# First layer's feed-forward by pairs of chunks, and the queries' weights loaded by blocks

## The chip, the cores and the metric

The kernel runs on one core of a Trainium2 chip, in one launch. All data are float32. The metric is the device time of an execution in microseconds (us). A profiled execution gives a trace besides: every instruction of every engine with its start and its duration. The engines are called by their short names here: PE (TensorE, the matrix products; PEld is its loading of weights), DVE (VectorE), ACT (ScalarE), POOL (GpSimd) and SP (SyncE, which mostly issues DMAs).

## The reference, cut to what matters

Two layers work on x of 4 x 512 tokens with 512 features. The change lies in the first one. Its normalised input xn goes two ways: through an attention that is a sequential scan over minibatches of 16 tokens (each step updates a small weight matrix by a gradient), and through a gated feed-forward. Both are added to x. The second layer has an attention with compressed keys and queries ("latents") and a feed-forward of four experts; it is not touched by the change itself.

```python
# first layer, attention: 32 heads of 16, one step for each of 32 minibatches
Z1 = xk @ W1_s + b1_s
grad = _ln_fused_l2_bwd(Z1, xv - xk, ln_w, ln_b)
Z1_bar = xq @ W1_s - eta_mb * Attn1 @ grad + b1_bar
W1_new = W1_s - (last_eta * xk).swapaxes(-1, -2) @ grad
# first layer, feed-forward: 512 -> 1408 -> 512
g = jnp.einsum('th,ih->ti', xf, gate_w) * gate_s
u = jnp.einsum('th,ih->ti', xf, up_w) * up_s
hdn = jax.nn.silu(g) * u
out = jnp.einsum('ti,hi->th', hdn, down_w) * down_s
# the whole
x = x + attention_0(xn) + ffn_0(xn)          # layer 0
x = x + attention_1(xn) + experts_1(xn)      # layer 1, with xn of the new x
```

## The kernel before

The first stage (some 930 us of the trace) does the whole first layer. It cuts the 512 tokens of each of the four batches into NCHUNK = 8 chunks of 64 tokens, so that a chunk has CW = 256 columns (64 tokens x 4 batches), and a chunk holds CH = 4 steps of the recurrence (NM = 32 steps in all, numbered n = 0 to 31 here).

The recurrence is the loop near the end of the stage (L781 to L797). Each step forms the products pz (first_product, L345) from the running weights, whose block-diagonal copy is wq_bd (L332). The gradient is a chain of small operations on DVE with a square and a square root on ACT (L354 to L390). Its result goes into g_bd (L395) for the products wacc that update the weights, and into gh (L421, POOL) for the products pso that give the step's output. The next step's pz needs wacc. All these PE products are short; in a step the gradient chain is what takes the time.

While that chain runs, PE gets other work. `work` is a chain of Python generators, one `between(ch)` for each chunk (L656 to L687). Each piece of work that such a generator emits gives back an estimate of its time, and `fill(us)` takes pieces until the estimates cover the given number of us. A step calls fill three times, with 11, 3 and 8 us (GAPS): before the update, before the output products, and after them. A further loop empties the generator as far as needed before the next chunk's first step, because that step needs the chunk's keys, tokens and queries (`done`). The order in which the program text emits instructions isn't the order that each engine gets: the framework's scheduler orders the instructions of an engine anew, by its own plan, when the program is built. Once built, the order on each engine is fixed.

The pieces of `between(ch)` are, in order:
- gate_up(ch, i) for 11 blocks of 128 hidden units (L465 to L481). Two weight tiles wg and wu of 256 KB each are loaded on SP (two buffers each). Four products of 256 columns each go into each half of the PSUM tile pf (ps_ff, two buffers). ACT makes sg = Silu of the first half (L477), DVE multiplies it with the other half into hid (L478). hid has one buffer.
- For the next chunk: norm_turn (transposes of the normalised rows into xT), keys, two token tiles (values and step sizes, stored as rows and read back as kv), and queries. keys and queries call `features` (L242), four output blocks of four products each; the queries' weights are one tile wq of 1 MB that stays in SBUF for the whole stage (L188).
- down(ch, u) for both halves of the chunk (L483 to L498): 11 products of 512 columns (pd) with one weight tile wd of 256 KB each, four buffers, loaded on SP.
- finish(ch - 1) (L545 to L606): gate the recurrence's outputs, norm them, project them, add everything up, norm again, transpose and store them (xe_d) for the second layer.

In the last chunk latent_operands, latent_rows and latents (L610 ff.) compute the second layer's latents: the normalised rows of chunks 0 to 5 are read back into the memory of wk, wv and wq (`latent_rows(k)`, L622 to L625), as soon as that memory isn't needed any more, those of chunks 6 and 7 stay in SBUF in xT tiles. After this stage come the expert feed-forward (L914 ff.; its weights gu and rows xe are issued on POOL at L927 and L931, more of them on SP) and the second attention, up to 2028 us.

Every f32 product leaves two records in the trace, so that counts of PE records are twice the counts of products.

## Time and profile before

| What | Value |
|---|---|
| three runs | 2028.45, 2035.72, 2035.77 us; median 2035.72 us |
| the profiled execution | 2030.29 us; span from first to last instruction 2028.3 us |
| mean granted TensorE clock | 0.998 |
| ACT busy | 863.2 us (43% of the span) |
| table loads of ACT in the first stage | 1.28 us each where they show |
| loads wg and wu (SP) | 88 each, 256 KB, 3.1 us from issue to landing (median) |
| loads wd (SP) | 176, 256 KB, 3.0 us |
| loads kv (POOL) | 32, 264 KB, 4.1 us |
| SP's data queue (q1) | 237.31 MB, 43.2% of 16 DMA engines |

How to read the profile: a row of the groups names line, engine, operation, `out<-in` by the program's names, tile sizes, the number of records, then the busy time in us and the mean duration in ns, then the idle time of the engine just before these instructions and what ended most of it. PE's products overlap, each is still draining when the next one streams, so that the mean of a record (388 ns) is longer than the distance between two of them. A row of the timeline begins with the start in us and the length of a run of like instructions; in brackets stands the idle time ahead of it and what released it. A row of the waits has the total in us, the number of waits and the longest.

Over the first stage, in slices of 100 us from the start, PE is busy for 89.1, 97.1, 95.0, 96.7, 94.5, 98.7, 97.8, 97.9 and 93.6 us.

### The profile page before, as it was taken

Reading aid. Unit: us, or ns where it says so; the run is one execution under the profiler, and the core shown is the slowest. Engines: PE = TensorE matmul, PEld = TensorE weight load, DVE = VectorE, ACT = ScalarE, POOL = GpSimd, SP = SyncE. Lnnn points to the kernel's source line nnn. Section 1 sums busy time; section 2 is a strip of 40 time slices with the busy share of each in tenths; the row PEclk is TensorE's granted clock in tenths of the full one; section 3 lists DMA queues with packets and bytes.
Section 4 is the critical chain, followed back from the end, with each engine's and each line's share of the span. In section 5 each row is a group of like instructions: output and inputs, shape, how many; then the busy total and the mean of one; then the engine's idle time right before and its main releaser. Section 6 shows DMA issues by size and latency. Waiting matters only on the chain.

```text
span 2028.3 us, 30787 instructions
## 1 busy us (share of the span) xinstructions
PE 1968.2 (97%) x10502; PEld 1245.2 (61%) x10502; DVE 1302.3 (64%) x2720; ACT 863.2 (43%) x1763; POOL 631.8 (31%) x707
## 2 busy tenths in 40 slices
PE   8999999999999999998999999999999999999999
PEld 6777676767676776744776445555555555555555
DVE  4546657575756574754654487777777777777773
ACT  2233343333343443422322365555555555555552
POOL 4334242434342433421001132223223232354320
PEclk9999999999999999999999999999999999999999
DMA  6757576646373655545831144344434443333332
GB/s 166 210 129 220 132 193 166 183 128 184 114 203 116 179 151 163 182 136 189 281 104 56 39 101 117 95 103 115 108 94 114 103 114 86 97 97 89 94 100 93
DMA packets 318472, 270.90 MB, mean 134 GB/s; under 512 B 87660, under 2 KB 239405, under 8 KB 317677
## 3 DMA queue, kind: packets, MB, share of 16 engines
q1 hardware_dynamic: 298080, 237.31, 43.2%
q0 software_dynamic: 8736, 26.31, 4.5%
q10 hardware_dynamic: 11500, 5.32, 0.9%
q8 instruction: 84, 1.38, 0.3%
q14 instruction: 72, 0.58, 0.1%
HBM read 174.18 MB, written 34.87 MB: 103 GB/s over the span
## 4 chain that ended last, share of the span: by engine, by line
PE 47%; DVE 1%; SPq 1%; ACT 1%; issue 0%; DMA 0%; DVEq 0%; ACTq 0%
PE sc L1134 9%; PE pc L1202 9%; PE pq L1124 7%; PE px L1245 5%; PE p L1245 4%; PE epg L969 3%; PE epo L1032 3%; PE pk L1116 2%; PE epu L969 1%; SPq L1194 1%; PE po L1302 1%; PE pw L868 1%; PE pvo L886 1%; ACT prob L1139 1%; ACT prob L1144 0%
## 5 line engine op out<-in xcount | busy, mean ns | idle before, releaser
L1139 ACT ACTIVATE prob<-sc,mx 128x512 f32<-128x512 f32 x256 | 174.3, 683 | 164.2 <-DVE mx L1136 159.4
L1134 PE MATMUL sc<-kT,qT 96*128 96x512 f32 x512 | 230.6, 592 | 1.6 <-DVE prT_head L1183 1.3
L1202 PE MATMUL pc<-prT,lv 128*128 128x512 f32 x488 | 219.6, 593 | 1.2 <-DMA prT<-tt 1.2
L1109 POOL TENSOR_TENSOR kT<-t_k,t_k 32x512 f32<-32x512 f32 x64 | 80.6, 1259 | 407.6 <-PE pq L1124 235.6
L1163 DVE STREAM_TRANSPOSE tt<-prob 128x512 f32<-128x512 f32 x248 | 170.3, 706 | 55.2 <-ACT prob L1144 43.7
L117 PE MATMUL pf<-xT,wg 128*128 128x256 f32 x704 | 173.7, 388 | 5.3 <-DMA wg<-in_wg 2.7
L1144 ACT ACTIVATE prob<-prob,sm 128x512 f32<-128x512 f32 x256 | 176.5, 713 | 0.0
L1124 PE MATMUL pq<-cq,uq 128*128 128x512 f32 x384 | 175.3, 592 | 0.8 <-ACT ctxT L1204 0.8
L1134 PEld LDWEIGHTS sc<-kT,qT 96*128 96x128 f32 x512 | 96.8, 190 | 124.1 <-issue 118.9
L1136 DVE TENSOR_REDUCE mx<-sc 128x1 f32<-128x512 f32 x256 | 168.0, 677 | 2.3 <-PE sc L1134 0.3
L117 PE MATMUL pf<-xT,wu 128*128 128x256 f32 x704 | 167.0, 380 | 1.3 <-DMA wu<-in_wu 1.3
L117 PE MATMUL pd<-wd,hid 128*128 128x512 f32 x352 | 165.9, 600 | 1.8 <-DMA wd<-in_wd 1.7
L117 PEld LDWEIGHTS pf<-xT,wg 128*128 128x128 f32 x704 | 132.1, 192 | 32.9 <-issue 7.6
L1202 PEld LDWEIGHTS pc<-prT,lv 128*128 128x128 f32 x488 | 92.5, 190 | 93.7 <-issue 90.7
L117 PEld LDWEIGHTS pf<-xT,wu 128*128 128x128 f32 x704 | 133.7, 190 | 20.4 <-DMA wu<-in_wu 2.3
L478 DVE SCALAR_TENSOR_TENSOR hid<-pf,us,sg 128x256 f32<-128x256 f32 x88 | 41.9, 477 | 153.9 <-ACT sg L477 153.5
L1124 PEld LDWEIGHTS pq<-cq,uq 128*128 128x128 f32 x384 | 72.8, 190 | 93.1 <-issue 81.5
L314 POOL TENSOR_SCALAR sk<-k,m 128x256 f32<-128x256 f32 x64 | 61.1, 964 | 179.8 <-PE pz L117 167.7
L421 POOL TENSOR_SCALAR gh<-grad,m 128x256 f32<-128x256 f32 x64 | 61.2, 967 | 153.2 <-DVE grad L390 135.5
L117 PEld LDWEIGHTS pd<-wd,hid 128*128 128x128 f32 x352 | 63.4, 190 | 60.5 <-issue 45.2
L1109 POOL TENSOR_TENSOR qT<-t_q,t_q 32x512 f32<-32x512 f32 x64 | 80.6, 1260 | 56.7 <-DVE t_q L1105 56.6
L477 ACT ACTIVATE sg<-pf,gs 128x256 f32<-128x256 f32 x88 | 41.5, 473 | 132.9 <-PE pf L117 132.5
(304 smaller groups left out, 3546.6 us busy)
## 6 DMA issues: line engine op xcount, KB each, us to landing
prT<-tt SPq DMA_DIRECT2D x992, 64.0 KB, 2.0
wd<-in_wd SPq DMA_DIRECT2D x176, 256.0 KB, 3.0
wg<-in_wg SPq DMA_DIRECT2D x88, 256.0 KB, 3.1
wu<-in_wu SPq DMA_DIRECT2D x88, 256.0 KB, 3.1
cq<-lat_d SPq DMA_DIRECT2D x48, 256.0 KB, 4.3
rows<-rows SPq DMA_DIRECT2D x128, 66.0 KB, 2.2
kv<-rows POOLq DMA_DIRECT2D x32, 264.0 KB, 4.1
gu<-in_gu SPq DMA_DIRECT2D x3, 2048.0 KB, 8.8
```

The costliest lines, as they stand in the source:

```text
L117: nc.tensor.matmul(out, lhsT=lhsT, rhs=rhs, start=start, stop=stop, skip_group_check=True)
L421: nc.gpsimd.tensor_scalar_mul(gh[:, :, h, :], g, m2[:, h : h + 1])
L969: nc.tensor.matmul(ps, lhsT=w[:, c, :], rhs=x[:, c], start=start and c == 0, stop=c == 1, skip_group_check=True)
L1109: nc.gpsimd.tensor_sub(t[RD:mid, :], t1[RD:mid, :], t2[RD:mid, :])
L1124: nc.tensor.matmul(pq, lhsT=w[f"uq{i}"][:, h, :], rhs=cqs[hg, b][:, i, :], start=(i == 0), stop=(i == nq - 1))
L1134: pin(nc.tensor.matmul(ps, lhsT=qT[:KQ, i * P : (i + 1) * P], rhs=kT[:KQ, :], start=True, stop=True))
L1136: pin(nc.vector.tensor_reduce(mx, ps, AX.X, ALU.max, negate=True))
L1139: pin(nc.scalar.activation(pr, ps, AF.Exp, bias=mx, scale=1.0, accum_out=sm))
L1144: pin(nc.scalar.mul(pr, pr, sm))
L1163: nc.vector.transpose(out=tt[:, :, :, i, :], in_=pr.rearrange("p (kb e j) -> p kb e j", e=2, j=K))
L1202: pin(nc.tensor.matmul(pc, lhsT=lv[:, b, k, :], rhs=prT[:, k, :], start=(k == 0), stop=(k == E - 1)))
L1245: nc.tensor.matmul(ps[:, q, :], lhsT=a[:, k, q * P : (q + 1) * P], rhs=w[:, k, :], start=start and k == 0 and q == 0, stop=k == 1, skip_gr ...
```

## The change

Gate and up products are made for a pair of chunks at a time, 512 columns a product. The tiles xT and hid hold pairs now (two xT buffers of a pair for three of a chunk; hid 22 KB a partition for 11), and pf is one tile for gate and one for up. An even chunk's `between` has nine of the pair's eleven blocks (FF_FIRST = 9), the projections of the next chunk and finish; an odd one has the other two blocks, the down products of both chunks, the projections and finish. The queries' weights no longer stay in SBUF: each chunk loads four blocks of 256 KB into the buffers of wg and wu, on SP. The buffers of kv and q1 go from three to two, those of sg from two to one. Of the latents, the rows of chunks 4 and 5 go into the memory of hid, and come last; the rows of chunks 6 and 7 share one tile.

```diff
--- before.py
+++ after.py
@@ -41,6 +41,8 @@
 
 INTER = 1408
 NI = INTER // P
+
+FF_FIRST = 9
 
 H, D, KVC, QC, RD = 16, 128, 128, 384, 64
 HALF = RD // 2
@@ -120,7 +122,7 @@
             return ps_pj.tile([P, 512], F32, tag="pj", name="pj")
 
 
-        xTs, xns = {}, {}
+        xTs, xTp, xns = {}, {}, {}
 
         def load_rows(t, src, ch, u):
             for b2 in range(2):
@@ -152,7 +154,9 @@
                 xns[ch, u] = xt
 
         def norm_turn(ch):
-            xTs[ch] = wk.tile([P, NC, CW], F32, tag="xT", name=f"xT{ch}", bufs=3)
+            if ch % 2 == 0:
+                xTp[ch // 2] = wk.tile([P, NC, 2, CW], F32, tag="xT", name=f"xT{ch}")
+            xTs[ch] = xTp[ch // 2][:, :, ch % 2, :]
             for u in range(2):
                 nc.scalar.copy(xTs[ch][:, :, u * P : (u + 1) * P], transposed(xns.pop((ch, u))))
                 yield 0.6
@@ -185,7 +189,6 @@
         gamma_row = wk.tile([P, HS], F32, tag="xr", name="gamma_row")
         gbeta_row = one.tile([P, HS], F32, tag="gbeta_row", name="gbeta_row")
         lrw = load(one, "lrw", [P, NC, P], a["lrw"].rearrange("(c p) m -> p c m", p=P))
-        wq_w = load(one, "wq", [P, NC, HS], a["wq"].rearrange("(c p) o -> p c o", p=P))
         one_row = one.tile([1, P], F32, tag="one_row", name="one_row")
         nc.vector.memset(one_row, 1.0)
 
@@ -239,21 +242,30 @@
         z_d = [dram.tile([NC * P, B, CT], F32, tag=f"z{ch}", name=f"z{ch}") for ch in range(NCHUNK)]
         k1, q1, rows = {}, {}, {}
 
-        def features(ch, w, got, tag, bufs):
-
-            t = got[ch] = wk.tile([P, NC, CW], F32, tag=tag, name=f"{tag}_{ch}", bufs=bufs)
+        def features(ch, w, got, tag):
+
+            t = got[ch] = wk.tile([P, NC, CW], F32, tag=tag, name=f"{tag}_{ch}", bufs=2)
             for be in range(NC):
                 pp = psum()[:, :CW]
+                wb = w(be)
                 for c in range(NC):
-                    mm(pp, w[:, c, be * P : (be + 1) * P], xTs[ch][:, c, :], c == 0, c == NC - 1)
+                    mm(pp, wb[:, c, :], xTs[ch][:, c, :], c == 0, c == NC - 1)
                 nc.scalar.copy(t[:, be, :], pp)
                 yield 1.72
 
         def keys(ch):
-            return features(ch, wk_w, k1, "k1", 2)
+            return features(ch, lambda be: wk_w[:, :, be * P : (be + 1) * P], k1, "k1")
 
         def queries(ch):
-            return features(ch, wq_w, q1, "q1", 3)
+            def block(be):
+
+                w = wk.tile([P, NC, P], F32, tag="wg" if be % 2 else "wu", name=f"wq_{ch}_{be}")
+                nc.sync.dma_start(
+                    out=w, in_=a["wq"].rearrange("(c p) o -> p c o", p=P)[:, :, be * P : (be + 1) * P]
+                )
+                return w
+
+            return features(ch, block, q1, "q1")
 
         def token_tile(ch, u):
             t = wk.tile([P, NS, RW], F32, tag="rows", name=f"rows_{ch}_{u}")
@@ -303,7 +315,7 @@
         def prepare(n):
 
             ch, i = divmod(n, CH)
-            kv = wk.tile([P, B, RW], F32, tag="kv", name=f"kv_{n}", bufs=3)
+            kv = wk.tile([P, B, RW], F32, tag="kv", name=f"kv_{n}")
             nc.gpsimd.dma_start(out=kv, in_=rows_d[ch][i].rearrange("s t b x -> (s t) b x"))
 
             def at(t, r):
@@ -462,21 +474,26 @@
         nc.gpsimd.dma_start(out=row["dsc"], in_=a["dsc"].unsqueeze(0))
         hid, yf = {}, {}
 
-        def gate_up(ch, i):
+        def gate_up(k, i):
+
             if i == 0:
-                hid[ch] = wk.tile([P, NI, CW], F32, tag="hid", name=f"hid_{ch}", bufs=1)
-            pf = ps_ff.tile([P, 2, CW], F32, tag="pf", name=f"pf_{ch}_{i}")
-            for j, nm in enumerate(("wg", "wu")):
-                w = wk.tile([P, NC, P], F32, tag=nm, name=f"{nm}_{ch}_{i}")
+                hid[k] = wk.tile([P, NI, 2, CW], F32, tag="hid", name=f"hid_{k}", bufs=1)
+            pf = []
+            for nm in ("wg", "wu"):
+                w = wk.tile([P, NC, P], F32, tag=nm, name=f"{nm}_{k}_{i}")
                 nc.sync.dma_start(out=w, in_=a[nm][i])
+                ps = ps_ff.tile([P, 2 * CW], F32, tag="pf", name=f"pf_{nm}_{k}_{i}")
+                pf.append(ps)
                 for c in range(NC):
-                    mm(pf[:, j, :], w[:, c, :], xTs[ch][:, c, :], c == 0, c == NC - 1)
-            if i < 10:
-                next(copies, None)
-            sg = wk.tile([P, CW], F32, tag="sg", name=f"sg_{ch}_{i}")
-            nc.scalar.activation(sg, pf[:, 0, :], AF.Silu, scale=gs[:, i : i + 1])
+                    mm(ps, w[:, c, :], xTp[k][:, c].rearrange("p h t -> p (h t)"), c == 0, c == NC - 1)
+                if i < 10:
+                    next(copies, None)
+                if nm == "wg":
+                    sg = wk.tile([P, 2 * CW], F32, tag="sg", name=f"sg_{k}_{i}", bufs=1)
+                    nc.scalar.activation(sg, ps, AF.Silu, scale=gs[:, i : i + 1])
+                    yield 3.43
             nc.vector.scalar_tensor_tensor(
-                hid[ch][:, i, :], pf[:, 1, :], us[:, i : i + 1], sg, ALU.mult, ALU.mult
+                hid[k][:, i].rearrange("p h t -> p (h t)"), pf[1], us[:, i : i + 1], sg, ALU.mult, ALU.mult
             )
             yield 3.43
 
@@ -487,7 +504,7 @@
             for i in range(NI):
                 w = wk.tile([P, HS], F32, tag="wd", name=f"wd_{ch}_{u}_{i}", bufs=4)
                 nc.sync.dma_start(out=w, in_=a["wd"][i * P : (i + 1) * P, :])
-                mm(pd, hid[ch][:, i, u * P : (u + 1) * P], w, i == 0, i == NI - 1)
+                mm(pd, hid[ch // 2][:, i, ch % 2, u * P : (u + 1) * P], w, i == 0, i == NI - 1)
                 if i in (3, 7):
                     yield 3.43
             t = wk.tile([P, HS], F32, tag="yf", name=f"yf_{ch}_{u}", bufs=4)
@@ -593,8 +610,9 @@
                 xns[ch, u] = xt
                 yield 4.4
             if ch >= NCHUNK - 2:
-                t = wk.tile([P, NC, CW], F32, tag="xT", name=f"xl_{ch}", bufs=3)
-                part = parts[ch] = t.rearrange("p c w -> p (c w)").rearrange("p (u c e x) -> p u c e x", u=2, c=NC, e=E)
+                if not last_rows:
+                    last_rows.append(wk.tile([P, 2, 2, NC, E, 32], F32, tag="xT", name="xl_last"))
+                part = parts[ch] = last_rows[0][:, ch % 2]
             for u in range(2):
                 if ch >= NCHUNK - 2:
                     xs = part[:, u]
@@ -605,7 +623,7 @@
                 yield 0.6
 
 
-        parts, lw = {}, []
+        parts, lw, last_rows = {}, [], []
 
         def latent_operands():
 
@@ -620,7 +638,12 @@
                 lw.extend(t[:, :, i * P : (i + 1) * P] for i in range(n // P))
 
         def latent_rows(k):
-            t = parts[2 * k, 2 * k + 1] = one.tile([P, 4, NC, E, 32], F32, tag=("wk", "wv", "wq")[k], name=f"xl_{k}")
+            if k < 2:
+                t = one.tile([P, 4, NC, E, 32], F32, tag=("wk", "wv")[k], name=f"xl_{k}")
+            else:
+                t = wk.tile([P, NI, 2, CW], F32, tag="hid", name=f"xl_{k}", bufs=1)
+                t = t[:, :4].rearrange("p i h t -> p (i h t)").rearrange("p (i c e x) -> p i c e x", i=4, c=NC, e=E)
+            parts[2 * k, 2 * k + 1] = t
             for i in range(4):
                 nc.sync.dma_start(out=t[:, i], in_=xe_d[4 * k + i])
 
@@ -656,36 +679,59 @@
         def between(ch):
 
             fin = finish(ch - 1) if ch > 0 else iter(())
-            if ch + 1 == NCHUNK:
+            k, odd = divmod(ch, 2)
+            proj = (keys(ch + 1), token_tile(ch + 1, 0), token_tile(ch + 1, 1), queries(ch + 1))
+            if not odd:
+                yield from norm_turn(ch + 1)
+                for i in range(FF_FIRST):
+                    yield from gate_up(k, i)
+                    if i == 3:
+                        yield from take(fin, 1)
+                if ch == 0:
+                    yield from finish_constants()
+                nxt = chain(*proj)
+                for j in range(6):
+                    yield from take(nxt, 2)
+                    yield from take(fin, 1)
+                yield from nxt
+                done.add(ch + 1)
+                yield from fin
+                if ch + 2 < NCHUNK:
+                    norm_rows(ch + 2)
+                return
+            last = ch + 1 == NCHUNK
+            if last:
                 latent_operands()
-            for i in range(NI):
-                yield from gate_up(ch, i)
-                if ch + 1 == NCHUNK and i in (2, 5, 8):
-                    latent_rows(i // 3)
-                if i == NI - 3:
-                    yield from take(fin, 1)
-            if ch == 0:
-                yield from finish_constants()
+                latent_rows(0)
+            for i in range(FF_FIRST, NI):
+                yield from gate_up(k, i)
+            if last:
+                latent_rows(1)
+            yield from down(ch - 1, 0)
+            yield from take(fin, 1)
+            dn = down(ch - 1, 1)
+            yield from take(dn, 2)
             nxt = iter(())
-            if ch + 1 < NCHUNK:
-                nxt = chain(
-                    norm_turn(ch + 1), keys(ch + 1), token_tile(ch + 1, 0), token_tile(ch + 1, 1), queries(ch + 1)
-                )
+            if last:
+                yield from dn
+                yield from fin
             else:
-                yield from fin
+                nxt = chain(norm_turn(ch + 1), *proj)
             for u in range(2):
-                dn = down(ch, u)
-                for j in range(3):
+                dn = chain(dn, down(ch, u))
+                for j in range(3 + (u == 0)):
                     yield from take(nxt, 2)
                     yield from take(dn, 1)
                     yield from take(fin, 1)
+                if u == 0 and ch + 2 < NCHUNK:
+                    norm_rows(ch + 2)
             yield from nxt
             done.add(ch + 1)
+            yield from dn
             yield from fin
-            if ch + 2 < NCHUNK:
-                norm_rows(ch + 2)
-            if ch + 1 == NCHUNK:
-                for key in sorted(parts, key=str):
+            if last:
+                latent_rows(2)
+                for key in ((0, 1), (2, 3), 6, (4, 5)):
                     yield from latents(key)
 
         def take(it, k):
```

## The prediction

> **What bounds the kernel now.** I read the page's busy times first, then the costliest groups, the waits of PE up to 930 us (the first stage), and last the PE, DVE and POOL timelines of single places.
>
> ```profile
> PE 1968.2 (97%) x10502; PEld 1245.2 (61%) x10502; DVE 1302.3 (64%) x2720; ACT 863.2 (43%) x1763; POOL 631.8 (31%) x707
> L117 PE MATMUL pf<-xT,wg 128*128 128x256 f32 x704 | 173.7, 388 | 5.3 <-DMA wg<-in_wg 2.7
> L117 PE MATMUL pf<-xT,wu 128*128 128x256 f32 x704 | 167.0, 380 | 1.3 <-DMA wu<-in_wu 1.3
> L117 PE MATMUL pd<-wd,hid 128*128 128x512 f32 x352 | 165.9, 600 | 1.8 <-DMA wd<-in_wd 1.7
> L478 DVE SCALAR_TENSOR_TENSOR hid<-pf,us,sg 128x256 f32<-128x256 f32 x88 | 41.9, 477 | 153.9 <-ACT sg L477 153.5
> ```
>
> PE is busy 97% of the span. The gate and up products (pf) and the down products (pd) hardly wait, and they are what PE does while the recurrence's gradient runs on DVE. So two things alone can move the time: how long PE needs for its products, and how much PE work stands ready inside each recurrence step. The waits show the second:
>
> ```profile
> PE pso L117 <- POOL gh L421: 5.6, 3, 2.7
> PE wacc L117 <- ACT g_bd L395: 3.5, 4, 1.6
> ...
> PE pf L117 <- DMA wg<-in_wg: 2.7, 2, 2.6
> PE pz L117 <- ACT wq_bd L332: 2.5, 2, 1.4
> ...
> PE pf L117 <- DVE hid L478: 2.2, 3, 1.1
> ```
>
> All waits of this view come to about 45 us, no more than that can be won by tidier waiting. Two steps of the recurrence are "thin", with less PE work than gradient; here they are as PE saw them:
>
> ```profile
> 263.60 0.48 PE L117 MATMUL pso<-a_bd,gh 128*32 128x68 f32 x17 [2.72 <-POOL gh L421]
> ...
> 266.78 1.08 PE L117 MATMUL pz<-wq_bd,sk 128*32 128x128 f32 x32 [1.40 <-ACT wq_bd L332]
> ...
> 268.24 1.99 PE L117 MATMUL pf<-xT,wg 128*128 128x256 f32 x8
> 270.07 1.89 PE L117 MATMUL pf<-xT,wu 128*128 128x256 f32 x8
> 271.80 1.89 PE L117 MATMUL pf<-xT,wg 128*128 128x256 f32 x8
> ```
>
> ```profile
> 701.98 1.08 PE L117 MATMUL pz<-wq_bd,sk 128*32 128x128 f32 x32
> ...
> 712.23 0.65 PE L117 MATMUL wacc<-g_bd,km 128*32 128x64 f32 x32 [1.61 <-ACT g_bd L395]
> ```
>
> From the end of pz (703.06) to wacc (712.23) is 9.2 us. DVE shows that this is the chain itself, with hardly a foreign operation in it:
>
> ```profile
> 703.13 0.42 DVE L356 TENSOR_REDUCE s<-pz 128x16 f32<-128x256 f32 x1
> ...
> 711.27 0.81 DVE L395 COPY g_bd<-grad 32x256 f32<-32x256 f32 x2
> ```
>
> In the thin step that ends at 263.6 the chain took 10.6 us, with two hid operations of the feed-forward (0.48 and 0.47 us) inside. I price it at 9.9, the middle, with 9.2 and 10.6 as ends.
>
> **Streaming.** Each f32 product has two records. In the fence that begins at 263.60, eight records of 256 columns follow eight others after 1.73 to 1.83 us (1.727 over the whole run of them), 0.216 us a record. For 512 columns:
>
> ```profile
> 303.61 3.60 PE L117 MATMUL pd<-wd,hid 128*128 128x512 f32 x8
> 307.04 0.59 PE L117 MATMUL pz<-gsum,bones 128*128 128x256 f32 x2
> ```
>
> Eight records take 3.43 us, 0.429 each. So a 512-wide product saves 2 x 1.727 - 3.43 = 0.024 us per four products; 88 such groups (four pairs, 11 blocks, two matrices) give **-2.1 us**. The Trainium skill (TensorE: Matmul & The Clock Gate, section "Back-to-back issue gap") has a sustained stream of load and matmul at about 81 ns for N = 128 and 131 ns for N = 512; drawn linearly, an estimate, 98 ns at 256. By that rule a 512 product costs 0.67 of two of 256, and the 173.7 + 167.0 us of pf would lose about 112 us. The row rules it out: here time goes with columns and the weight load (190 ns) is already under the 213 ns of the pass. I take -2.1, ends 0 and -4.
>
> **Thin steps (the largest term).** The change orders work anew: even chunks hold nine gate/up pairs, odd ones two, then 2 x 2 down tiles. I counted, in the built order of PE, the fill that stands between pz of each step and its first wacc, at 0.43 us a 512-wide record and 0.216 a 256-wide one, plus 0.6 for the queries' pso:
> - step 3: queries' blocks 2 and 3 (3.4) and four down products (3.4), 6.9; missing 9.9 - 0.6 - 6.9 = 2.4.
> - step 7: one block of queries (1.7) and eight transposes (1.0), 2.7; missing 6.6.
> - step 15: 8.6; missing 0.7.
> - step 28 (first of the last chunk): only the two 512-wide bones products, 1.7, because the next gate product stands behind wacc; missing 7.6.
>
> That is 17.3. After wacc there is nothing before the next pz in steps 3 and 7 (1.4 each, the wait in the line at 266.78) and 0.9 us in steps 11 and 15 (0.5 each): 3.8. Sum 21.1. The thin steps of before (2.72 + 1.40 above, 1.05 of another pz, 1.61) are gone, -6.8: **+14.3**. With 9.2 it is +11.5, with 10.6 about +17. All other steps keep 8.9 us or more of fill in both orders. These steps are late because the next minibatch needs wacc; nothing else is ready on PE.
>
> **Waits on gate loads and hid.** The waits of pf in this view (2.7 for wg, 1.3 for wu, 2.2 for hid, 0.4 for a buffer freed late behind xh, 6.6 in all) belong to blocks; half as many blocks give **-3.3** (0 to -6.6). A rule speaks against the wider operations: the Trainium skill (Perfetto Trace Analysis, "Optimizing Scalar/DVE Operations") says that where ScalarE or VectorE aren't saturated but make bubbles elsewhere, breaking instructions up may let work finish sooner. Silu and hid go from 0.47 us (their rows) to about 0.68 (the 128x512 rows of ACT in the attention). By the rule each pair would pay 0.2 us more bubble, 44 x 0.2 = +9. But the page shows hid waiting for sg 153.5 us in all and PE waiting for hid 2.2: a pf buffer comes free while PE streams 3.43 us of the other one, in both kernels. I take the row.
>
> **The start.** In the two orders, 6.9 us of pf stood among the startup's products before the first pz, now 1.0 us of transposes, so that the first pz comes 4.9 us earlier and about 1 us of cover is lost. **+1** (0 to +2).
>
> **Queries by blocks.** 32 loads of 256 KB are added, 88 gate/up loads go (176 to 88); all on SP's queue, which gets shorter (q1 is busy 43%). Block 0 is covered by some 7 us of token-tile products against a landing of 3.1. Cost 0; uncovered, 3 us per chunk. kv and q1 with two buffers in place of three: kv lands in 4.1 us and is asked for one step (some 25 us) ahead, so 0; if a load came a whole landing late each time it would be 30 x 4.
>
> **Down in long runs.** Odd chunks have up to 14 to 20 down products in a row. A product needs 0.857 us of PE and one 256 KB load; four buffers over 0.857 + 0.33 (issue) + 3.0 (landing) give 1.05 us each. Before, runs of 8 and 10 lost 0.9 and 1.8 us. **+3** (0 to +6).
>
> **Tail.** Rows 4 and 5 of the latents move into the hid tile and come last. The final norm's transposes lose 3.2 + 0.7 us of cover and 1.3 us of existing waits go: **+2.3**. The expert weights overlay the same memory, so they are moved as well:
>
> ```profile
> 910.97 0.75 POOL L927 DMA_DIRECT2D gu<-in_gu  x1
> ...
> 923.49 0.54 POOL L931 DMA_DIRECT2D xe<-xe_d  x1 [7.05 <-DMA gu<-in_gu]
> ```
>
> gu and 14 xe loads on POOL, and two xe with gu_1, dn and y behind them on SP, now wait for the last latent product; adding up the products that stand before it in both orders puts the last xe about 17.7 us later. PE needed them at 969.35; by the same count the first epg moves by 18.5 to 22 us (the sum below and the tail's own). **+1** (0 to +6).
>
> **Sum.** 14.3 - 2.1 - 3.3 + 1 + 3 + 2.3 + 1 = +16.2 us. The profiled run took 2030.29 us (span 2028.3 and 2.0 around it); so 2046.5. The median of the three runs, 2035.72, is 5.4 above the profiled run, the lowest 1.8 below, so a scatter of some 5 us lies on either side.
>
> **Rivals.**
> 1. *Evens out* (2032). The thin steps cost as before because chain and fill overlap better than counted, and the tail hides: half the thin term (+7), -2.1, -3.3, nothing else. For it: POOL and ACT have slack everywhere. Against: fill is counted from a fixed order.
> 2. *Faster* (2020). Half as many Silu and hid operations, each with its wait, and 65 table loads in place of 83 in the built order (1.28 us each in the trace) shorten the waits everywhere: half of the 38 us outside the thin steps go (-19), -2.1, thin steps at the short chain (+11.5): -9.6. It decides when over 22 us of the 45 go, or when the thin steps cost under some 2 us. Against: most of these 38 us are norms and loads that are not changed.
> 3. *Slower by much more* (2066). The tail's loads come too late for the experts: gu takes 12 us and xe 9 us to land; if the first expert product waits for both, +20 in place of +1. It decides from the point where xe issue later than 9 us before epg. The kv of the last chunk, needed about when its rows are stored (13.5 us against 14.3), would add here.
> 4. *The change doesn't do what it says*: the built order shows 512-wide products and single blocks; none given.
>
> **Numbers.** Forecast 0.56 (own range 2036 to 2060), evens out 0.18, faster 0.15, much slower 0.11. Half a per cent, about what a measurement can tell from no change, is 10 us. Slower: most of the forecast (0.52) and rival 3, 0.63; same: rival 1 and the forecast's edge, 0.22; faster 0.15. The range takes 2023 to 2064.
>
> **What will show it.** pf records of about 592 ns, spaced 0.43, 704 in all. Waits of wacc for g_bd (or pso for gh) of 6 to 8 us near the first chunk's end (step 7) and in step 28; pz for wq_bd 1.4. Waits of pd for wd of a few us. The issue of gu against the first epg. It is wrong if thin steps show no wait over 3 us, if pf's records are spaced under 0.4 us, or if waits of the unchanged norms grow.

## The result and the profile after

| Kernel | Median | Ratio to before, 95% interval |
|---|---|---|
| before | 2035.49 us (4 runs beside it) | 1 |
| changed | 2101.37 us (2099.95 to 2103.43) | 1.0334 (1.0322 to 1.0347) |

The change makes the kernel 3.3% slower, some 66 us, where 16 were forecast and 2064 was the upper end of the range. The profiled execution of the changed kernel took 2099.95 us (span 2098.2). In it the first expert product (epg) starts at 1038.33 us, in the kernel before at 969.35; these 69.0 us are practically the whole loss (the spans differ by 69.9). So nearly all of it lies in the first stage.

The profile page of the changed kernel, the rows that answer to those shown of before:

```profile
PE 1989.9 (95%) x9798; PEld 1122.0 (53%) x9798; DVE 1300.1 (62%) x2676; ACT 830.2 (40%) x1701; POOL 632.8 (30%) x707
...
PEclk9999989999999999899999999999999999999999
...
L119 PE MATMUL pd<-wd,hid 128*128 128x512 f32 x352 | 171.9, 612 | 16.3 <-DMA wd<-in_wd 11.1
L119 PE MATMUL pf_wg<-xT,wg 128*128 128x512 f32 x352 | 169.9, 627 | 12.8 <-ACT sg L493 12.8
...
L119 PE MATMUL pf_wu<-xT,wu 128*128 128x512 f32 x352 | 159.8, 597 | 2.0 <-DVE hid L495 2.0
```

Two things stand out. Idle time before pd has gone from 1.8 to 16.3 us, and pf now waits 12.8 us for Silu (sg), a wait that the list of before doesn't have. And the mean granted clock, 0.998 before, is 0.981 here. (The groups pf_wg and pf_wu have half the records, each twice as wide; the 597 ns of a pf_wu record is close to the forecast 592.)

The waits of PE up to 1000 us (total, number, longest):

```profile
PE pso L119 <- POOL gh L433: 24.9, 4, 14.2
PE pf_wg L119 <- ACT sg L493: 12.8, 3, 8.6
PE pd L119 <- DMA wd<-in_wd: 11.1, 12, 2.6
PE pj L119 <- ACT pn_sq L566: 8.4, 1, 8.4
PE pd L119 <- DVE yf L511: 5.2, 3, 3.0
...
PE pz L119 <- POOL wq_bd L328: 3.0, 1, 3.0
```

To split the 69.0 us I took the windows view in slices of 1 us up to the first epg, added up the part of each slice in which PE was idle, and, for the part in which it was busy, its length times (1 - granted clock):

| up to the first epg | before | changed | difference |
|---|---|---|---|
| PE idle | 46.9 us | 94.2 us | +47.3 |
| PE busy, lost to a lower clock | 3.3 us | 24.6 us | +21.3 |
| PE busy, the rest | 919.1 us | 919.6 us | +0.5 |
| sum, rounded | 969.35 us | 1038.33 us | +69.0 |

Two thirds are stalls, one third is time at a lower clock, which comes behind stalls. The PE work itself has not got shorter by being wider.

**Late operands from POOL.** The worst stalls stand in the first step of chunks 3, 5 and 7 (steps 12, 20, 28). Two names are needed for them: zb is the recurrence's output of the chunk before, stored as z and read back, and pn_sq is the first operation of its norm. Step 12 on PE, then on DVE, ACT and POOL:

```profile
392.80 1.08 PE L119 MATMUL pz<-wq_bd,sk 128*32 128x128 f32 x32
...
395.22 3.60 PE L119 MATMUL pf_wg<-xT,wg 128*128 128x512 f32 x8
398.65 3.60 PE L119 MATMUL pf_wu<-xT,wu 128*128 128x512 f32 x8
410.81 6.36 PE L119 MATMUL pf_wg<-xT,wg 128*128 128x512 f32 x8 [8.56 <-ACT sg L493]
```

```profile
402.75 0.18 DVE L379 TENSOR_TENSOR rl<-r,kv 128x16 f32<-128x16 f32 x1 [3.71 <-DMA kv<-rows]
...
406.93 0.90 DVE L407 COPY g_bd<-grad 32x256 f32<-32x256 f32 x2
```

```profile
406.85 1.06 ACT L566 ACTIVATE pn_sq<-zb 128x1024 f32<-128x1024 f32 x1 [3.16 <-DMA zb<-z]
407.93 0.83 ACT L407 COPY g_bd<-grad 32x256 f32<-32x256 f32 x2
408.77 1.28 ACT L493 ACT_TABLE_LOAD   x1
410.07 0.69 ACT L493 ACTIVATE sg<-pf_wg,gs 128x512 f32<-128x512 f32 x1
```

```profile
395.23 1.11 POOL L319 DMA_DIRECT2D kv<-rows  x2
396.39 0.84 POOL L328 COPY wq_bd<-q 32x256 f32<-32x256 f32 x2
402.39 0.76 POOL L468 DMA_DIRECT2D zb<-z  x1 [5.17 <-DMA z<-zch]
```

Read from the stall backwards. PE had fill in its queue (the next gate product), but no free pf buffer: Silu of the first was late. ACT hadn't been slow; in its order Silu stands behind pn_sq and the g_bd copies. (Silu's one buffer in place of two, which no run has alone, is not it: ACT waits for it 1.4 us in the whole stage.) The copies wait for DVE's gradient, and DVE stood for 3.71 us for kv; pn_sq waits for zb. The two came within a tenth of a us of each other (gradient 406.89, zb 406.85), so that here either alone would have held ACT nearly as long. Both loads come late from POOL: zb waits there for the landing of z, and kv was issued only at 395.23, while this step's pz had started at 392.80. The fence on ACT shows as well why fill in a queue isn't always fill: it needs buffers that come free on other engines.

In steps 20 and 28 the issues came at 631.63 and 867.88, 5.8 and 4.7 us after their pz, and DVE stood for 5.91 and 4.62 us. PE in steps 20 and 28, then POOL in step 28:

```profile
635.75 3.78 PE L119 MATMUL pj<-pn_sq,bones 128*128 128x512 f32 x4 [8.41 <-ACT pn_sq L566]
...
863.17 1.08 PE L119 MATMUL pz<-wq_bd,sk 128*32 128x128 f32 x32
...
880.78 0.32 PE L119 MATMUL pso<-a_bd,gh 128*32 128x68 f32 x1 [14.17 <-POOL gh L433]
```

```profile
864.47 1.82 POOL L326 TENSOR_SCALAR sk<-k,m 128x256 f32<-128x256 f32 x2 [1.63 <-PE pz L119]
866.24 1.69 POOL L328 COPY wq_bd<-q 32x256 f32<-32x256 f32 x4
867.88 1.16 POOL L319 DMA_DIRECT2D kv<-rows  x2
```

The program text asks for kv ahead of sk (L319, L326). The built order has it behind an sk that itself waits for this step's pz, so that kv can't be asked for before the step has begun. In the kernel before, kv of step 20 was issued 2 us ahead of its pz:

```profile
591.15 1.11 POOL L307 DMA_DIRECT2D kv<-rows  x2
```

```profile
593.11 1.08 PE L117 MATMUL pz<-wq_bd,sk 128*32 128x128 f32 x32
```

The place of the issue isn't all. In the windows around steps 12, 20 and 28 kv landed 7.7, 5.7 and 6.0 us after its issue (3.6 is the median of all), while the DMA engines were 92, 86 and 100% busy over some 6 to 8 us from the issue on. With the 4.1 us that the prediction took, DVE would have stood for some 0.3, 4.3 and 2.9 us, an estimate from the times above, in place of 3.71, 5.91 and 4.62: about half is late issue, the rest slow landing. No run separates the two.

The two runs of eight gate and up records at step 12 start 3.43 us apart, as forecast for 512 columns; the eight at 410.81 take 6.36 us. The windows view around steps 12 and 28 (PE busy, PEld, DVE, ACT, POOL, granted clock, DMA share, GB/s):

```profile
395.00:405.00 10.00, 7.25 (x17) 2.85 (x15) 5.79 (x17) 2.30 (x4) 4.64 (x8) 1.00 0.88 296
405.00:415.00 10.00, 4.19 (x5) 1.85 (x6) 3.98 (x8) 3.83 (x5) 7.57 (x10) 0.55 0.19 64
870.00:880.00 10.00, 0.00 (x0) 0.00 (x0) 5.62 (x11) 2.08 (x3) 5.79 (x7) 0.51 0.53 189
880.00:890.00 10.00, 9.22 (x29) 4.46 (x30) 0.08 (x1) 0.69 (x1) 0.73 (x1) 0.81 0.00 0
```

After a stall PE works at half its clock for some us more. In half-us slices, PE's last product before the stall of step 28 ends near 866.6, the clock is at 0.50 from about 870.2 and back at 1.00 from about 883.8, 3 us after work had begun again at 880.78. The Trainium skill (TensorE: Matmul & The Clock Gate, section "What's actually happening") has half rate after an idle window of about 3.4 us and full rate after a busy one. This stall agrees, with 3.6 and 3.0 us; shorter ones don't all (last section). The prediction left the clock out.

### The profile page after: what moved, and what is told of

The parts are those of the page before. It is cut to its first block, busy times and chain, and to the rows that moved or that the text cites. A ratio compares the mean times of both kernels' runs of the same rounds, so it can differ in the third digit from the quotient of the medians.

```text
span 2098.2 us, 29227 instructions
## 1 busy us (share of the span) xinstructions
PE 1989.9 (95%) x9798; PEld 1122.0 (53%) x9798; DVE 1300.1 (62%) x2676; ACT 830.2 (40%) x1701; POOL 632.8 (30%) x707
## 4 chain that ended last, share of the span: by engine, by line
PE 77%; DVE 9%; DMA 6%; ACT 3%; issue 2%; SPq 1%; POOL 1%; ACTq 0%; DVEq 0%; POOLq 0%
PE pj L119 10%; PE sc L1180 9%; PE pc L1248 9%; PE pq L1170 7%; PE pf_wg L119 7%; PE pf_wu L119 6%; PE px L1291 5%; PE pd L119 4%; PE p L1291 4%; PE epg L1015 3%; PE epo L1078 3%; PE pk L1162 2%; PE pz L119 2%; PE epu L1015 1%; DMA wd<-in_wd 1%
## 5 line engine op out<-in xcount | busy, mean ns | idle before, releaser
L119 PE MATMUL pd<-wd,hid 128*128 128x512 f32 x352 | 171.9, 612 | 16.3 <-DMA wd<-in_wd 11.1
L119 PE MATMUL pf_wg<-xT,wg 128*128 128x512 f32 x352 | 169.9, 627 | 12.8 <-ACT sg L493 12.8
L119 PE MATMUL pf_wu<-xT,wu 128*128 128x512 f32 x352 | 159.8, 597 | 2.0 <-DVE hid L495 2.0
L119 PEld LDWEIGHTS pf_wg<-xT,wg 128*128 128x128 f32 x352 | 69.3, 201 | 98.6 <-issue 82.0
L495 DVE SCALAR_TENSOR_TENSOR hid<-pf_wu,us,sg 128x512 f32<-128x512 f32 x44 | 32.9, 748 | 141.3 <-PE pf_wu L119 135.4
L119 PEld LDWEIGHTS pf_wu<-xT,wu 128*128 128x128 f32 x352 | 65.6, 190 | 82.0 <-issue 75.8
L326 POOL TENSOR_SCALAR sk<-k,m 128x256 f32<-128x256 f32 x64 | 60.0, 948 | 162.6 <-PE pz L119 132.3
L333 POOL TENSOR_SCALAR km<-kv,m2n 128x256 f32<-128x256 f32 x64 | 62.3, 982 | 126.9 <-PE wacc L119 110.5
```

The source lines that it names most:

```text
L119: nc.tensor.matmul(out, lhsT=lhsT, rhs=rhs, start=start, stop=stop, skip_group_check=True)
```

## The experiments

My theory after this profile: the new order of the work makes queries and kv late at chunk ends; the stalls follow from that, and the clock from the stalls. The rivals: the width itself, the pairs with their uneven chunks, the two buffers of kv, the 32 loads as such.

**1. Width undone** (time per column or per product?)

```diff
-                for c in range(NC):
-                    mm(ps, w[:, c, :], xTp[k][:, c].rearrange("p h t -> p (h t)"), c == 0, c == NC - 1)
+                for h in range(2):
+                    for c in range(NC):
+                        mm(ps[:, h * CW : (h + 1) * CW], w[:, c, :], xTp[k][:, c, h, :], c == 0, c == NC - 1)
```

> The changed kernel with each 512-wide gate and up product made as two of 256 columns (8 products a block and matrix in place of 4), all else as changed. The changed kernel's median is 2101.4. My theory (time on PE goes with columns; the loss comes from the order of the work and the stalls it brings): +2 us, 2099 to 2107. If the width itself brought a gain[...]: about +110 us. If wide pieces were what hurts (ScalarE and VectorE operations of 512 columns stay here, only PE's pieces differ): no change either, so a clear gain would speak for a third cause.

Measured: 2098.5 us, ratio 1.0326 (1.0303 to 1.0349). No difference from the changed kernel that can be told (the intervals overlap), certainly not 110 us. Columns cost, products don't; the width of PE's products neither gains nor harms by more than some 5 us.

**2. kv issued on another queue**

```diff
-            nc.gpsimd.dma_start(out=kv, in_=rows_d[ch][i].rearrange("s t b x -> (s t) b x"))
+            nc.sync.dma_start(out=kv, in_=rows_d[ch][i].rearrange("s t b x -> (s t) b x"))
```

> The changed kernel with the loads of kv issued on SP in place of POOL, where they stood behind the next step's sk and wq_bd. My theory (in the first step of chunks 3, 5 and 7 kv is asked for 2.4 to 5.8 us after the step's pz, and VectorE stands still for 3.7, 5.9 and 4.6 us, and with it the Silu and PE's fill): VectorE's waits for kv fall from 18.5 to under 6 us, PE's waits of 8.6 and 8.4 us and half of the one of 14.2 go, with three falls of the clock: 2070 to 2082. Rival (the thin places of PE's order alone cost the time, and kv is late only where PE had nothing to do anyway): over 2093.

Measured: 2071.2 us, ratio 1.0189 (1.0165 to 1.0213). One changed word takes 30 us back. DVE's waits for kv no longer show in its list (18.5 us in the changed kernel), PE's idle time up to epg is 70.1 us for 94.2, and the clock loss 15.6 for 24.6. At step 12 the stall has hardly shrunk; a wait of 7.40 us for sg is left, and the row on ACT says why:

```profile
396.52 1.06 ACT L566 ACTIVATE pn_sq<-zb 128x1024 f32<-128x1024 f32 x1 [6.07 <-DMA zb<-z]
```

With kv in time zb alone holds ACT, and Silu behind it. At step 20 the 8.41 us became 4.57, again for pn_sq. At step 28 the 14.17 us are gone, but there the built order of PE changed too (12.0 us of fill by count ahead of wacc, 1.7 in the changed kernel). So the 30 us aren't the price of late kv alone; what is shown is that the place of one load's issue, and the order that the planner makes around it, is worth 30 us.

**3. The stalls filled with useless products.** In four steps products are added whose results nobody reads; the rest is as changed.

```diff
+KEEP = {7: 13, 12: 12, 20: 17, 28: 30}
...
+            if n in KEEP:
+                pk = psum()
+                for _ in range(KEEP[n]):
+                    mm(pk[:, :CW], ident, sq.rearrange("p g d -> p (g d)"))
```

> The changed kernel with products that nobody reads added on PE in steps 7, 12, 20 and 28, right behind the gradient's square (13, 12, 17 and 30 products of 256 columns, 5.6, 5.2, 7.3 and 12.9 us), in the place where PE stood idle. They give no useful work. If the halved clock after a stall costs time of its own (my reading: 21 of the 69 us): the falls of the clock after these four stalls, worth 2.7 + 2.7 + 2.9 + 1.5 = 9.8 us of PE time, go: 2088 to 2095. If the clock only goes with the stalls and costs nothing beside them: 2100 or more, by what the added products delay.

Measured: 2091.9 us, ratio 1.0293 (1.027 to 1.0316). More work, and 9.5 us less time. The windows of step 12 with it:

```profile
395.00:405.00 10.00, 8.01 (x20) 3.50 (x19) 6.86 (x15) 4.12 (x6) 8.60 (x11) 1.00 0.48 141
405.00:415.00 10.00, 10.00 (x43) 4.29 (x45) 0.94 (x2) 1.97 (x2) 1.33 (x2) 1.00 0.34 100
```

The clock stays at 1.00 where it was 0.55, and the loss to the clock in the whole stage falls from 24.6 to 9.0 us. PE idles 29.2 us less and is busy 33.1 us more (full-speed time), so that the added products by themselves cost about 4 us. Apart from them PE's order is nearly that of the changed kernel, so the gain is the clock's. The lower clock costs time of its own. (DVE still waits 17.3 us for kv here: this mends the consequence, not the cause.)

**4. Projections early.** In even chunks the pieces of the next chunk's projections come two after each gate/up pair; the pieces of finish move with them.

```diff
+                nxt = chain(*proj)
                 for i in range(FF_FIRST):
                     yield from gate_up(k, i)
...
+                    yield from take(nxt, 2)
...
-                nxt = chain(*proj)
-                for j in range(6):
-                    yield from take(nxt, 2)
-                    yield from take(fin, 1)
                 yield from nxt
```

> The changed kernel with the projections of an even chunk's successor (keys, token tiles, queries) mixed among the nine gate/up pairs, two pieces after each pair, in place of all behind the ninth pair. PE's order then has fill missing for 5.6 us by my count, against 21.9 in the changed kernel and 7.7 in the kernel before, and kv can be loaded a step ahead. My theory (late projections make the thin steps and the late kv): nearly all of the loss goes, 2025 to 2050. Rival (pairs hurt by the width of their pieces, the double load of down products in odd chunks and the tail): 2070 or more.

Measured: 2047.2 us, ratio 1.0071 (1.0045 to 1.0098). 54 of the 66 us come back by order alone, with pairs and blocks kept; DVE waits for no kv, PE's idle time up to epg is 55.2 us, and 6.8 are lost to the clock. What is left has another shape. PE's waits in this run:

```profile
PE pd L119 <- DMA wd<-in_wd: 15.2, 18, 2.6
PE pso L119 <- POOL gh L433: 10.9, 4, 4.5
PE pd L119 <- DVE yf L511: 4.0, 3, 1.6
```

The down products wait for their weights; the runs of them have got longer (lengths under experiment 7).

**5. The blocks alone, in the kernel before.** Single chunks, 256 columns, queries' weights by blocks.

```diff
...
         def queries(ch):
-            return features(ch, wq_w, q1, "q1", 3)
+            def block(be):
+                w = wk.tile([P, NC, P], F32, tag="wg" if be % 2 else "wu", name=f"wq_{ch}_{be}")
...
+            return features(ch, block, q1, "q1", 3)
```

> The kernel before with one part of the change alone: the queries' weights loaded by four blocks of 256 KB a chunk into the gate/up buffers, on SP, in place of the 1 MB that stays. Chunks stay single and products 256 wide. By my count of PE's order 25 us more fill is missing than before (steps 3, 7, 11, 15 and 28), and kv is issued later. My theory (the blocks share the gate/up buffers, so the planner puts queries late, and the thin steps of the changed kernel come from this): 25 us of stalls and some four falls of the clock of 1.5 to 2.7: 2055 to 2080. Rival (the pairs' uneven chunks, with projections all at an even chunk's end, make the late queries, and the blocks cost nothing): 2030 to 2040.

Measured: 2091.4 us, ratio 1.0287 (1.0263 to 1.0311). More than I expected: this part alone costs 58 us, with everything that marks the changed kernel: 89.1 us idle, 21.3 lost to the clock, DVE waiting 18.2 us for kv. Steps 3 and 7 on PE:

```profile
157.45 0.32 PE L117 MATMUL pso<-a_bd,gh 128*32 128x68 f32 x1 [10.06 <-POOL gh L429]
...
274.84 0.32 PE L117 MATMUL pso<-a_bd,gh 128*32 128x68 f32 x1 [8.01 <-POOL gh L429]
```

**6. Two buffers of kv and q1 alone, in the kernel before.**

```diff
-            kv = wk.tile([P, B, RW], F32, tag="kv", name=f"kv_{n}", bufs=3)
+            kv = wk.tile([P, B, RW], F32, tag="kv", name=f"kv_{n}", bufs=2)
...
-            return features(ch, wq_w, q1, "q1", 3)
+            return features(ch, wq_w, q1, "q1", 2)
```

> The kernel before with two buffers in place of three for kv and for the queries' result q1. PE's order is the same instruction for instruction. My theory (the buffer count isn't what makes kv late in the changed kernel, the place of its issue on POOL is): no change, within 0.3% of before. Rival (with two buffers kv is loaded a step later and arrives late at the first steps of chunks): 10 to 30 us slower.

Measured: 2040.6 us, ratio 1.004 (1.0028 to 1.0052). Neither: kv isn't late (DVE waits 1.9 us for it), but 7 us are lost. The load's issue itself now waits for the buffer, on POOL, and what stands behind it there waits as well:

```profile
POOL kv L307 <- DVE pair L379: 33.7, 9, 8.2
```

In the kernel before this row is 1.1 us, once. pn_sq, whose input zb is issued on POOL too, keeps PE waiting for 11.2 us in place of 6.3. Most of the loss is the clock again: the first epg comes 8.1 us later, of which 2.4 are idle time and 5.8 a lower clock (over all runs the mean granted clock is 0.9933, in the runs of before beside them 0.9959). One of the new falls follows a 3.19 us wait for pn_sq (up to 187.81), ahead of which POOL waited 2.86 us for a kv buffer before it issued zb. The longest wait for pn_sq, 5.0 us up to 928.84, has no wait for a kv buffer ahead of it; its cause stays open.

**7. Shorter runs of down products,** on top of experiment 4: in odd chunks one piece of the projections between two pieces of down.

```diff
-            yield from down(ch - 1, 0)
...
+            nxt = iter(()) if last else chain(norm_turn(ch + 1), *proj)
+            dn = chain(down(ch - 1, 0), down(ch - 1, 1), down(ch, 0), down(ch, 1))
+            for j in range(12):
+                yield from take(nxt, 1)
+                yield from take(dn, 1)
+                if j > 1:
+                    yield from take(fin, 1)
```

> The last kernel with early projections, and in its odd chunks one piece of the projections between each two pieces of down products, in place of five pieces of down in a row ahead of them. The longest runs of down products in PE's order become 25, 11, 11, 9 for 28, 27, 25, 23; the missing fill is 4.9 us by count for 5.6. My theory (long runs outrun the loads of wd, 15.2 us of waits in that kernel and 1.7 in the kernel before, since each product of 0.86 us needs 256 KB): waits for wd under 8 us, 2030 to 2042. Rival (wd is late because of what else SP issues, wherever down stands): within 4 us of 2047.

Measured: 2052.7 us, ratio 1.0093 (1.0069 to 1.0117). The waits for wd fell only to 11.4 us, and the time did not fall: other waits (pn_sq 8.0) and the clock (18.0 lost for 6.8) took it. The rival's time, within 4 us of 2047, is missed as well. Run lengths are a part of the wait for wd at most. The blocks aren't the rest, since without them (experiment 12) pd still waits 10.1 us for wd; what delays these loads is open.

**8. and 9. Early projections in the kernel before,** two pieces a block from the fifth on, then one piece from the sixth on.

```diff
+            nxt = iter(())
+            if ch + 1 < NCHUNK:
+                nxt = chain(
+                    norm_turn(ch + 1), keys(ch + 1), token_tile(ch + 1, 0), token_tile(ch + 1, 1), queries(ch + 1)
+                )
             for i in range(NI):
                 yield from gate_up(ch, i)
...
+                if i >= 4:
+                    yield from take(nxt, 2)
```

In the second run the last two lines have `i >= 5` and `take(nxt, 1)`.

> The kernel before with the next chunk's projections mixed among its eleven gate/up blocks (two pieces after each block from the fifth on) in place of behind them. By count 1.2 us of fill are missing for 7.7, but down products stand in longer runs (18, 18, 13, 11 for 11, 9, 8, 8). If the lesson (projections ahead of the last gate/up work) holds without pairs: 5 to 10 us faster than before, 2023 to 2030. If longer runs of down cost as much as the thin steps did: 2030 to 2040.

> The kernel before with the next chunk's projections mixed among the gate/up blocks, one piece after each block from the sixth on (the run with two pieces a block was 2040.3, with 14.0 us of waits for wd in runs of up to 18 down products). Here part of the projections stays between the down products, whose longest runs are 13, 11, 6; missing fill 6.5 us by count, before 7.7. If the runs of down are what took back the gain: 2024 to 2034. If early projections cost something else: 2036 to 2044.

Measured: 2040.3 us, ratio 1.0033 (1.002 to 1.0047), and 2044.1 us, ratio 1.0052 (1.0039 to 1.0066). Both are slower than before. In the first, PE waits for wd 14.0 us, though its idle time in all is only 3.0 us above that of before. In the second it waits for wd only 4.5, and yet it isn't faster: g_bd and gh keep PE waiting for 19.2 us, for 11.0 before. My count of missing fill, 1.2 and 6.5 us for 7.7 before, foretold neither; it takes each step's chain to be equally long, which may be why. No version found here beats the kernel before.

**10. Blocks in buffers of their own,** in the kernel before (kv and q1 with two buffers, so that they fit; experiment 6 is what it stands against).

```diff
-                w = wk.tile([P, NC, P], F32, tag="wg" if be % 2 else "wu", name=f"wq_{ch}_{be}")
+                w = wk.tile([P, NC, P], F32, tag="wqb", name=f"wq_{ch}_{be}", bufs=2)
```

> The kernel before with the queries' weights by blocks, as in the run that had this part alone (2091.4), but in two buffers of their own in place of the gate/up buffers; kv and q1 have two buffers to make room (the run with that alone: 2040.6). The loads are the same 32 of 256 KB. Count of missing fill: 10.7 us, against 32.8 with shared buffers and 7.7 before. My theory (it is the sharing of the gate/up buffers that makes the planner put the queries late, and kv with them): 2038 to 2055. Rival (the loads as such, 32 more on SP, make the queries late): over 2075.

Measured: 2060.2 us, ratio 1.0129 (1.0112 to 1.0147). In between: of the 58 us some 20 stay (2060.2 against 2040.6). Sharing the gate/up buffers is the larger part, not all. What stays shows in one row: PE's pz waits 26.9 us for wq_bd from POOL (2.5 in experiment 6, for ACT), nearly all of it at the first steps of chunks 5, 6 and 7. PE, POOL and ACT at the first of these:

```profile
604.29 1.94 PE L117 MATMUL pz<-wq_bd,sk 128*32 128x128 f32 x32 [8.14 <-POOL wq_bd L324]
```

```profile
602.54 1.69 POOL L324 COPY wq_bd<-q 32x256 f32<-32x256 f32 x4 [4.53 <-ACT q L250]
```

```profile
600.89 1.06 ACT L557 ACTIVATE pn_sq<-zb 128x1024 f32<-128x1024 f32 x1 [10.89 <-DMA zb<-z]
601.86 0.63 ACT L250 COPY q<-pj 128x256 f32<-128x256 f32 x2
```

The queries' results stand on ACT behind pn_sq, which waits 10.89 us for a load that has nothing to do with them. At the other two (9.78 and 8.20 us) ACT has the same order, and POOL has the copies behind km besides, which waits 6.11 and 6.34 us for kv.

**11. Experiments 4 and 2 together.**

> The changed kernel with early projections (2047.2 alone) and the loads of kv on SP (2071.2 alone). With projections early kv is no longer late, so moving its issue should bring little more: what it still can bring is POOL's standing still for a kv buffer ahead of z and zb (up to 7.3 us each in the changed kernel's trace). My theory: 2040 to 2050. If lateness of kv still cost what it did in the changed kernel, the two gains would add up: 2017.

Measured: 2053.6 us, ratio 1.0109 (1.0086 to 1.0131), with its four runs spread from 2041 to 2060. The gains of 54 and 30 us don't add up, as expected, but the time lies above my 2040 to 2050, and no better than experiment 4 alone. With early projections DVE waits for no kv even when POOL issues it, so that there the place of the issue had nothing left to win.

**12. and 13. The blocks taken back in the changed kernel.** wq is resident again; yf, xt and xs have fewer buffers to make room. Beside it the control with the same smaller buffers and the blocks kept.

```diff
+        wq_w = load(one, "wq", [P, NC, HS], a["wq"].rearrange("(c p) o -> p c o", p=P))
...
-            return features(ch, block, q1, "q1")
+            return features(ch, lambda be: wq_w[:, :, be * P : (be + 1) * P], q1, "q1")
...
-            t = wk.tile([P, HS], F32, tag="yf", name=f"yf_{ch}_{u}", bufs=4)
+            t = wk.tile([P, HS], F32, tag="yf", name=f"yf_{ch}_{u}", bufs=2)
...
```

> The changed kernel with the queries' weights resident again (one 1 MB tile, as before), pairs and all else kept; to make room yf has two buffers in place of four, xt three for four, xs two for three. Missing fill by count 4.0 us, against 21.9 in the changed kernel. My theory (the blocks in the gate/up buffers are what turned the order bad, 58 us when alone in the kernel before): 2040 to 2060, with kv no longer late. Rival (the pairs with their uneven chunks do as much harm by themselves): over 2080.

> The control of the run beside it: the changed kernel with the same smaller buffers (yf two, xt three, xs two), the queries' weights by blocks as in the change. Both theories: 2095 to 2115, near the changed kernel's 2101; what it adds to 2101 is what the smaller buffers cost in the run beside it.

Measured: 2065.6 us, ratio 1.0162 (1.0145 to 1.0179), and 2108.5 us, ratio 1.0371 (1.0356 to 1.0387). The difference between the two is 43 us: what the blocks cost inside the changed kernel. The first lies 6 us above the time I gave it; the control shows that the smaller buffers cost about 7 us. DVE waits 2.7 us for kv. If these parts simply add up, which no run shows, the pairs without blocks and without smaller buffers would stand near 2101 - 43 = 2058 us, some 23 to 25 above before. These are the pairs' own, with the two buffers of kv (7 when alone) and the waits of down products (13.5 us of idle time in the first of the two runs, 1.8 before) among them; no run takes them apart further.

## Why the prediction was wrong

The direction was right, and so was the place; the size was a quarter of what came. The prediction opened with "two things alone can move the time", PE's own work and the fill in each step. Two others did: operands that came late from other engines, and PE's clock.

- **Streaming, -2.1: the mechanism right.** 3.43 us for eight records of 512, and experiment 1. The 112 us that it had estimated, and set aside, don't exist here. PE's work outside the clock loss changed by +0.5 us, so that even the 2.1 can't be seen.
- **Thin steps, +14.3: the right steps, and nearly the right sizes.** Step 3: 2.71 us of stall (2.4 forecast); step 7: 6.34 (6.6); step 15: none (0.7); pz waits of 3.0 in all (3.8), though at step 24. Step 28: 14.17 for 7.6, because there the chain itself was stretched by 4.62 us of DVE's waiting for kv. In all 26.2 - 6.8 = +19.4.
- **Queries by blocks and two kv buffers, "Cost 0": the step that failed.** The prediction priced the blocks by whether PE's work covers their loads, and there it was right: PE waits for no wq block. It priced kv by "asked for one step (some 25 us) ahead". That did not hold at the first steps of chunks even before, where kv of step 20 was issued 2 us ahead of its pz and kv of step 28 2.5 us behind it (810.42, pz 807.94). In the changed order kv of steps 12, 20 and 28 is asked for 2.4 to 5.8 us after the step has begun, and it lands in 5.7 to 7.7 us in place of 4.1. The built order of POOL has it behind the last step's copies, an sk and the issues of z and zb; the prediction's count took PE's order alone. Its "all other steps keep 8.9 us or more of fill" counted products in steps 12 and 20 that couldn't start, one for want of a pf buffer, the other for want of pn_sq. These two steps paid 8.56 + 8.41 us, with kv and zb both late from POOL, and step 28 some 6.6 us more than forecast. By experiment the blocks cost 58 us alone (5) and 43 in place (12, 13), the two kv and q1 buffers 7 (6), each with its share of the clock. The prediction did see kv's danger, for the last chunk only, and put it into the rival "slower by much more"; that rival's own reason, the experts' loads, did not come.
- **The clock: a term not in the sum at all, +21.3.** The trace of before had two such falls (slices near 55 and 816 us, 3.3 us lost), too small to catch the eye. Step 7's stall of 6.34 us cost another 2.7 us by the fall behind it.
- **Waits on gate loads and hid, -3.3: half right.** The waits for wg and wu are gone, hid's is 2.0 for 2.2; but Silu brought 12.8, 8.56 of them at step 12. And the waits for pn_sq grew from 6.7 to 9.9 us, a growth in the unchanged norms, which the prediction had named as a sign of being wrong.
- **Down in long runs, +3 (0 to 6): too small.** 11.1 us for wd and 5.2 for the one PSUM buffer of pd that DVE has to empty (yf), against 1.7 and nothing; +14.5. I had 1.05 us a product from the median landing of 3.0; the landing of wd is 3.3 in the changed kernel, and experiment 7 says that the runs aren't all of it; the rest stays open.
- **Tail, +2.3 and +1: right in kind.** The transposes wait 2.73 us for x. The expert loads cost nothing: the wait for t_ops at the first experts is 0.99 us, before 1.02.

Thin steps +19.4, steps 12 and 20 +17.0, down products +14.5 come to 50.9 us, against 47.3 us more idle time in all; other waits became 3.6 less. With the clock's 21.3 and 0.5 that is the 69 us.

## What to carry to other kernels

A load's cost isn't only whether PE's work covers it, but what its place does to the fixed order on every queue: read each in-order queue (here POOL and ACT) for what now stands ahead of the next critical operand. Where PE feeds a recurrence, charge a stall of about 3 us or more a second time, for the clock after it: in the traces of before, of the changed kernel and of experiment 6, each stall of 2.99 us or more after the start was followed by a fall, and a fall cost 1.5 to 3.4 us. Widening products that already cost by the column gained nothing here, and the memory for it was not free: fewer buffers cost 7 us each time (experiment 6, and the control of 12).

## What the runs showed that I had not expected

A shorter stall can bring the clock down too: PE was idle for 2.35 us up to 285.21 us, and its clock was at 0.50 from about 286.5 to 289.9, while it was busy again. The fall came 3.6 us after PE's last product, as in step 28. It doesn't always: stalls of 2.55, 2.72 and 2.88 us in the kernel before, and one of 2.61 here, brought none. What decides between these is open. The same eight records that take 3.60 us took 5.40 there:

```profile
285.21 5.40 PE L119 MATMUL pf_wg<-xT,wg 128*128 128x512 f32 x8 [2.35 <-ACT sg L493]
```

Useless products on PE made the kernel 9.5 us faster (experiment 3). And two buffers in place of three, which left PE's order untouched, cost 7 us, in part at least by way of another engine's queue (experiment 6).
